# Eighteen full tiles of the first choice worked right behind attention, in a fused attention and mixture-of-experts block on Trainium2

## The chip, the cores and the metric

The kernel runs on one core of one Trainium2 chip. That core has TensorE (PE, with its weight load shown as PEld), VectorE (DVE), ScalarE (ACT), GpSimd (POOL) and SyncE (SP), and 16 DMA engines. PE multiplies, DVE, ACT and POOL work elementwise, SP and POOL issue most DMAs here. Each engine runs its own instructions in order, and waits at semaphores for the others. The metric is the device time of one execution in microseconds (us); less is better.

## The reference

The input x is 16 batches (B) of 512 tokens (L) with 128 channels (C). What is computed:

```
mod = (silu(c) @ wmod)                      # six vectors of 128 for each batch: sa ca ga sb cb gb
ga, gb = sign(.) * max(|.|, 0.25)
h = layernorm(x) * (1 + ca) + sa
x = x + ga * attention(h)                   # gather-conv: 8 heads, 32 taps each at learned offsets
h = layernorm(x) * (1 + cb) + sb
scores = h @ gate_w.T                       # 8 experts
the two best scores of each token, softmax over the two
y = sum over the two: share * ((silu(h1) * h2) @ w3[e].T),  h1, h2 = halves of h @ w12[e].T
x = x + gb * y
```

Only the two chosen experts of a token have to be worked. The kernel gathers each expert's tokens, and works the first choices of all tokens ("lo") before the second choices ("hi").

## The kernel before

**Attention.** The 16 batches are four groups (g) of four. A group has four head pairs (q) and two pairs of batches (p); a "cell" is one (g, q, p), 32 in all, and each takes nine steps. `attention()` writes out the order of the instructions by hand (no scheduler moves them): in each step it issues the cell's own work, and `between(s)` then places side work from four lists, `preparing`, `making`, `sorting` and `putting`, as far as the step's "room" in each engine lasts. The last cells are those of group 3.

**Dispatch.** What follows attention for a pair of batches is a `Dispatch` object. `make` is the out-projection (`multiply`, L1051), the residual (`add`, L1064), the second layernorm (`moments`, `root`, `scale`, `modulate`). `sort` transposes the result (L1109), multiplies by the gate weights (`scores`, L1115), ranks the eight scores (`ranks`, L1130 to L1142), picks two, computes their shares with a sigmoid, counts the tokens of each expert (`count`, PE) and adds them to the running count `run` (`places`): so each token has a row number in its expert's region, and pairs of batches must be counted one after another. `puts` are indirect DMAs on POOL's queue (`put`, L1225 to L1232), 128 rows each: for each pair of batches 8 to `lo_d` (130 numbers a row: share, place of the second choice, h) and 8 to `hi_d` (386 numbers: h, x, gb, share, token).

The pairs come out of attention in order. The last two are the pairs of group 3: the last but one ("pair 0") is made and sorted beside the last cells, as far as it gets, and the last (`last`) only after the last cell's `yg` (L989), whose rows it reads through `yl` (L1026). Behind attention stand, in this order: what is left of pair 0's sort, its 16 puts, the last pair's make and sort, its 16 puts, and `tile_table()` (L1303), 25 small DVE operations.

**Tiles.** An expert's rows are cut into tiles of 256 (MT). `tile_table` turns the counts into two tables of 38 entries (NTL) for lo and for hi: the row at which a tile begins and its expert, in `tab`, and the number of rows at its start to be skipped, in `sk` (a tile that would go past an expert's rows begins earlier and overlaps the one before).

**Experts.** The loop at the end of the kernel runs over pairs of tiles (TW = 2): 19 steps of lo, then 19 of hi. In a step: `front` has SP read a tile's address from the table and load its rows from `lo_d` or `hi_d` (one step ahead, L1569 to L1573); `load_lo` (hi only, L1582) loads the lo results from `yh_d`; `hidden` (L1613 to L1619) is the first product, silu and the gating; `turn` (L1600) transposes the next step's rows; `weights` has ACT copy the next step's two experts' weights; `output` (L1627) is the second product; `put_out` multiplies by the share and puts four times 128 rows out through indirect DMAs on POOL's queue (L1656): to `yh_d` in lo, to `out` in hi, after adding the lo results, gb and x. Rows, weights and results lie in a pool (`moe`) that is opened after attention's pool is closed.

For the program's semaphores, a DMA at an address read at run time counts as touching the whole of `lo_d`, `hi_d` or `yh_d`: a row load waits for all puts ahead of it in the program, and a put for all row loads ahead of it. The puts are written through separate views, so that they do not wait for one another.

## Time and profile before

| | us |
|---|---|
| median of 10 runs | 1428.37 (1421.17 to 1437.51) |
| the profiled execution | 1423.52 |
| its span (first to last instruction) | 1421.8 |
| PE busy, whole span | 1089.1 (77%) |
| DVE busy | 1083.5 (76%) |
| POOL busy | 808.0 (57%) |
| ACT busy | 739.8 (52%) |
| attention's last `yg` ends | 1117.0 |
| the first row load of lo is issued | 1167.7 |
| the steady steps of lo | 1185 to 1290 |
| the steady steps of hi | 1310 to 1405 |

The page gives busy times of each engine over the span, the granted TensorE clock as a share of full speed, and groups of instructions by line. The groups of the parts that matter here:

```profile
L1613 PE MATMUL hp<-h,wcp 128*128 128x256 f32 x608 | 140.9, 385 | 0.7 <-ACT h L1602 0.7
L1656 POOL DMA_INDIRECT yh_d<-o,to x76 | 74.7, 982 | 49.6 <-issue 17.7
L1656 POOL DMA_INDIRECT out<-o,to x76 | 74.9, 986 | 43.6 <-DVE o L1653 23.5
L1228 POOL DMA_INDIRECT lo_d<-wrow,at x64 | 64.2, 1004 | 47.5 <-issue 24.1
L1228 POOL DMA_INDIRECT hi_d<-wrow,at x64 | 63.5, 992 | 15.0 <-issue 14.3
```

A row reads: line, engine, operation, output and inputs, count, then busy time and mean nanoseconds of one, then the idle time of the engine just before these instructions and what ended most of it. Busy time of a DMA instruction on POOL is that of its issue; the data lands later. All times in the views below are from the span's start.

### The profile page before, as it was taken

Reading aid. Unit: us, or ns where it says so; the run is one execution under the profiler, and the core shown is the slowest. Engines: PE = TensorE matmul, PEld = TensorE weight load, DVE = VectorE, ACT = ScalarE, POOL = GpSimd, SP = SyncE. Lnnn points to the kernel's source line nnn. Section 1 sums busy time; section 2 is a strip of 40 time slices with the busy share of each in tenths; the row PEclk is TensorE's granted clock in tenths of the full one; section 3 lists DMA queues with packets and bytes.
Section 4 is the critical chain, followed back from the end, with each engine's and each line's share of the span. In section 5 each row is a group of like instructions: output and inputs, shape, how many; then the busy total and the mean of one; then the engine's idle time right before and its main releaser. Section 6 shows DMA issues by size and latency. Waiting matters only on the chain.

```text
span 1421.8 us, 21081 instructions
## 1 busy us (share of the span) xinstructions
PE 1089.1 (77%) x6422; PEld 460.1 (32%) x6422; DVE 1083.5 (76%) x1875; ACT 739.8 (52%) x1418; POOL 808.0 (57%) x851
## 2 busy tenths in 40 slices
PE   4377878886888788787888768877777419997995
PEld 2111212111222222212222222222212318996994
DVE  6587788787699889888899987878788743443775
ACT  5256655664564555654665545453544116564652
POOL 5555644443554386537844484754858354664666
PEclk9598999999998799879998998978988859998998
DMA  3353443444444333343344334443344223344772
GB/s 85 78 124 95 105 98 109 99 121 105 114 98 105 82 96 95 105 117 86 108 87 123 95 106 105 127 119 94 94 98 162 77 86 95 89 126 132 220 229 69
DMA packets 246863, 154.81 MB, mean 109 GB/s; under 512 B 169062, under 2 KB 217040, under 8 KB 246494
## 3 DMA queue, kind: packets, MB, share of 16 engines
q1 hardware_dynamic: 232300, 124.43, 33.9%
q0 software_dynamic: 13472, 28.37, 5.7%
q8 instruction: 51, 0.84, 0.3%
q10 hardware_dynamic: 978, 0.67, 0.2%
q14 instruction: 62, 0.51, 0.1%
HBM read 90.31 MB, written 64.09 MB: 109 GB/s over the span
## 4 chain that ended last, share of the span: by engine, by line
DVE 29%; PE 27%; issue 12%; ACT 11%; POOL 10%; DMA 7%; SPq 4%; POOLq 0%; ACTq 0%; DVEq 0%
DVE w L906 9%; DVE xx L908 8%; ACT n L870 6%; PE v L895 5%; PE hp L1613 4%; PE y L918 4%; POOL yh_d L1656 3%; PE v L866 3%; DMA wrow<-mod_d 3%; PE kp L513 2%; PE po L1627 2%; DVE ct L954 1%; PE kc L936 1%; ACT kc L888 1%; POOL nk L872 1%
## 5 line engine op out<-in xcount | busy, mean ns | idle before, releaser
L872 POOL TENSOR_SCALAR nk<-n 128x1024 int16<-128x1024 uint8 x256 | 270.8, 1058 | 399.1 <-ACT n L870 394.3
L870 ACT ACTIVATE n<-v 128x1024 uint8<-128x1024 f32 x256 | 261.9, 1023 | 291.8 <-PE v L866 282.7
L906 DVE SCALAR_TENSOR_TENSOR w<-v,kc 128x1024 f32<-128x1024 f32 x256 | 311.3, 1216 | 110.1 <-PE v L895 95.4
L908 DVE SCALAR_TENSOR_TENSOR xx<-v,w 128x1024 f32<-128x1024 f32 x256 | 313.4, 1224 | 8.8
L918 PE MATMUL y<-xx,dz 128*32 128x512 f32 x1024 | 300.5, 668 | 12.3 <-DVE xx L908 12.1
L918 PE MATMUL y<-w,zi 128*32 128x512 f32 x1024 | 302.4, 668 | 0.0
L895 PE MATMUL v<-nk,negn 128*128 128x512 f16 x512 | 174.3, 426 | 114.6 <-ACT n L870 83.1
L888 ACT COPY kc<-kt 128x128 f32<-128x128 f32 (+1 forms) x288 | 142.8, 496 | 162.4 <-DVE w L906 154.4
L866 PE MATMUL v<-rw,vt 32*128 32x512 bf16 x576 | 120.0, 413 | 63.2 <-DVE xx L908 61.0
L895 PEld LDWEIGHTS <-negn 128*128 128x128 bf16 x512 | 31.1, 99 | 351.4 <-ACT n L870 258.2
L1613 PE MATMUL hp<-h,wcp 128*128 128x256 f32 x608 | 140.9, 385 | 0.7 <-ACT h L1602 0.7
L1619 DVE TENSOR_TENSOR hid<-sl,hp 128x512 f32<-128x512 f32 x76 | 52.1, 686 | 116.9 <-ACT sl L1618 116.9
L1613 PEld LDWEIGHTS hp<-h,wcp 128*128 128x128 f32 x608 | 114.4, 194 | 15.9 <-ACT h L1602 1.1
L1656 POOL DMA_INDIRECT yh_d<-o,to x76 | 74.7, 982 | 49.6 <-issue 17.7
L1656 POOL DMA_INDIRECT out<-o,to x76 | 74.9, 986 | 43.6 <-DVE o L1653 23.5
L866 PEld LDWEIGHTS <-vt 32*128 32x128 bf16 x576 | 28.3, 92 | 202.7 <-DVE xx L908 96.4
L1228 POOL DMA_INDIRECT lo_d<-wrow,at x64 | 64.2, 1004 | 47.5 <-issue 24.1
L1618 ACT ACTIVATE sl<-hp 128x512 f32<-128x512 f32 x76 | 45.4, 597 | 87.0 <-PE hp L1613 87.0
L513 PE MATMUL kp<-hT,kw 128*128 128x512 f32 x128 | 80.3, 717 | 6.5 <-ACT cn L945 5.1
L1627 PE MATMUL po<-wcp,hid 128*128 128x128 f32 x608 | 76.1, 279 | 1.0 <-DVE hid L1619 1.0
L1627 PEld LDWEIGHTS po<-wcp,hid 128*128 128x128 f32 x608 | 72.7, 196 | 1.6 <-DVE hid L1619 1.5
L1228 POOL DMA_INDIRECT hi_d<-wrow,at x64 | 63.5, 992 | 15.0 <-issue 14.3
(272 smaller groups left out, 1655.9 us busy)
## 6 DMA issues: line engine op xcount, KB each, us to landing
row<-hi_d SPq DMA_DIRECT2D x38, 386.0 KB
kd<-ev SPq DMA_DIRECT2D x56, 256.0 KB
zi<-z_d SPq DMA_DIRECT2D x128, 64.0 KB
y_d<-yg SPq DMA_DIRECT2D x31, 256.0 KB
yl<-y_d SPq DMA_DIRECT2D x120, 64.0 KB
row<-lo_d SPq DMA_DIRECT2D x38, 130.0 KB
yl<-yh_d SPq DMA_DIRECT2D x38, 128.0 KB
xin<-in_x SPq DMA_DIRECT2D x8, 512.0 KB
```

The costliest lines, as they stand in the source:

```text
L866: T.matmul(v[:, n, :], vt[g, j, :], self.rw[n][g], start=True, stop=True)
L870: S.activation(n8, v, AF.Relu)
L872: G.tensor_scalar(self.new, n8, 64.0, 64.0, ALU.mult, ALU.add)
L888: S.copy(self.kc.rearrange("p n (c r) -> p n c r", r=BW)[:, :, :, r0 : r0 + nr], src)
L895: T.matmul(self.v[:, n, :], negn, prev[:, n, :].bitcast(F16), start=False, stop=True, skip_group_check=True,)
L906: V.scalar_tensor_tensor(w, v, -0.5, self.kc, ALU.is_gt, ALU.mult)
L908: V.scalar_tensor_tensor(xx, v, TIE + 0.5, w, ALU.add, ALU.mult)
L918: T.matmul(self.y[o : o + 32], self.zt[n][k][:, r, :], m[:, n, :], start=(r == 0), stop=(r == BW - 1), skip_group_check=True,)
L1228: G.indirect_dma_start(views[name][self.b0 * NT + k], bass.IndirectOffsetOnAxis(ap=self.at[:, s, k : k + 1], axis=0), self.w[n][:, i, o : ...
L1613: T.matmul(hp[:, m, here], t["wc"][w][:, o : o + P], hT[:, here], start=True, stop=True, skip_group_check=True,)
L1627: T.matmul(po[:, i, :], hid[:, n, i * P : (i + 1) * P], t["wc"][i // MI][:, o : o + C], start=(n == 0), stop=(n == FF // P - 1),)
L1656: G.indirect_dma_start(dst, bass.IndirectOffsetOnAxis(ap=at[:, i, :], axis=0), o[:, i, :], None, bounds_check=(E * REG - 1, B * L - 1)[ph] ...
```

## The change

After twelve batches (three groups) are sorted, some tiles of the first choice are already full with rows of those batches. A second, smaller table (`early_table`) is computed when the third group's last pair is sorted, inside attention: it lists the first 18 (EARLY) such tiles. Right behind attention nine steps of lo run on these 18 tiles (`experts` with `beside_early`), and the last pair's make, the sorts of the last two pairs and the lo puts of pair 0 are placed among them in pieces, at two places in each step, by lists and "room" as in attention. What is left in the lists is then issued in one go (`drain`): the rest of the last pair's sort, `tile_table`, its 8 lo puts. Then the other ten steps of lo run (`experts` with `beside_rest`), with the 16 hi puts of the last two pairs (a new list, `far`) among them, and at the end the 19 steps of hi. Row loads are issued two steps ahead in place of one. The lo steps' buffers are taken over from tiles of attention; the `moe` pool, now for hi alone, is opened after the last lo step. `tile_table` subtracts the tiles that `early_table` used, counted in `used`, and is cut into four pieces. The bodies of `front`, `load_lo`, `weights`, `turn`, `hidden`, `output` and `put_out` (now `puts_out`) are the same but for where their tiles lie.

```diff
+EARLY = 18
...
+    tail = []
+
+    def dtile(name):
+
+        return ps_y.tile([P, L], FP, tag="y", name=name) if tail else mtile(name)
+
...
-                Work(lambda n=n, k=k: self.multiply(n, k), 6 * int(n == k == 0), pe=0.8, dve=0.4)
+                Work(lambda n=n, k=k: self.multiply(n, k), 0 if last else 6 * int(n == k == 0), pe=0.8, dve=0.4)
...
-            if last:
-                for n in range(2):
-                    out += [Work(lambda n=n: self.scale(n, True))]
-                    out += [Work(lambda n=n, k=k: self.modulate(n, k, e)) for k in range(2)]
-                    out += [Work(lambda n=n: self.transpose(n)), Work(lambda n=n: self.scores(n))]
...
-        def puts(self):
+        def puts(self, which=(0, 1)):
             return [
                 Work(lambda k=k, s=s: self.put(k, s), int(k == s == 0), pool=1.3)
-                for s in range(2) for k in range(2 * NT)
+                for s in which for k in range(2 * NT)
...
+    def early_table():
+
+        fl = const.tile([P, 1, E], FP, name="fl")
+        box = {}
+
+        def first():
+            area.extend([cell.tile([P, 2 * NT * E * E], FP, tag="ge", name="ge", bufs=1), 0])
+            V.memset(used, 0.0)
+            cnt = const.tile([P, 1, E], FP, name="cnta")
+            V.tensor_tensor(cnt, run[:, 0:1], reg0[:, 0:1], ALU.subtract)
+            whole(fl, cnt, 0.0)
+
+        def second():
+            upto = box["upto"] = ends_of(fl, 1)
+            here = used[:, 0:1]
+            V.tensor_tensor(here, fl, upto, ALU.subtract)
+            V.tensor_scalar(here, here, float(EARLY), 0.0, ALU.add, ALU.max)
+            V.tensor_tensor(here, here, fl, ALU.min)
+
+        def third():
+            ef, sums = regions(box["upto"][:, 0], 0, EARLY)
+            bs = sk[:, 0, 0:EARLY]
+            sums(bs, fl[:, 0, 0 : E - 1])
+            V.tensor_tensor(bs, kf[:, 0:EARLY], bs, ALU.subtract)
+            V.tensor_scalar(bs, bs, float(MT), None, ALU.mult)
+            V.scalar_tensor_tensor(bs, ef, float(REG), bs, ALU.mult, ALU.add)
+            V.tensor_copy(tab[:, 0, 0, 0:EARLY], bs)
+            V.tensor_copy(tab[:, 0, 1, 0:EARLY], ef)
+            V.memset(bs, 0.0)
+            area.clear()
+
+        return [Work(first, dve=0.9), Work(second, dve=1.2), Work(third, dve=2.0)]
...
+        def tiles(s):
+            o = (EARLY, 0)[s]
+            n = NTL - o
+            sks = sk[:, s, o:NTL]
+            ef, sums = regions(box["upto"][:, s], o, n)
+            sums(sks, dt[:, s])
+            V.tensor_tensor(sks, kf[:, 0:n], sks, ALU.subtract)
+            V.tensor_scalar(sks, sks, used[:, s, 0:1], float(MT), ALU.add, ALU.mult)
+            bs = table_tile("bs", n)
+            sums(bs, dc[:, s])
+            V.tensor_scalar(bs, bs, cnt[:, s, 0:1], -float(MT), ALU.add, ALU.add)
+            V.scalar_tensor_tensor(bs, bs, 0.0, sks, ALU.max, ALU.min)
+            V.tensor_tensor(sks, sks, bs, ALU.subtract)
+            V.scalar_tensor_tensor(bs, ef, float(REG), bs, ALU.mult, ALU.add)
+            V.tensor_copy(tab[:, s, 0, o:NTL], bs)
+            V.tensor_copy(tab[:, s, 1, o:NTL], ef)
+
+        return [Work(first, dve=1.1), Work(second, dve=1.1)] + [
+            Work(lambda s=s: tiles(s), dve=3.0) for s in range(2)
+        ]
...
+            sorting.items += d.sort()
+            if (g, p) == (NG - 2, NP - 1):
+                sorting.items += early_table()
+
+            def goes():
+                putting.items.extend(d.puts((0,) if ahead else (0, 1)))
+                if ahead:
+                    far.items.extend(d.puts((1,)))
+                put_done.append(d)
+
+            sorting.items += [Work(goes)]
...
+    def front(ph, k):
+
+        width = (2 + C, 3 * C + 2)[ph]
+        t = dict(ph=ph, k=k, wc=[], at=[])
+        row = t["row"] = (
+            after[0].tile([P, NT, width], FP, tag="row1", name="row1", bufs=6) if ph else lo["row"][k % 4]
+        )
...
+    def buffers():
+
+        h, kt = groups[-1].hT.rearrange("p b c r -> p (b c r)"), kts[1].rearrange("p s n t -> p (s n t)")
+        last_pr = prm.rearrange("p t q r -> p (t q r)").bitcast(FP)
+        kc = cell.tile([P, 2, L], FP, tag="kc", name="rowa", bufs=1).rearrange("p n l -> p (n l)")
+        m, wide = NT * (2 + C), 2 * FF + FF // P * C
+        lo["row"] = [
+            t.rearrange("p (i w) -> p i w", i=NT) for t in [h[:, m * n : m * n + m] for n in range(3)] + [kc[:, 0:m]]
+        ]
+        lo["wc"] = [kt[:, wide * n : wide * n + wide] for n in range(5)] + [last_pr[:, 0:wide]]
+        lo["x"] = [cell.tile([P, 2, L], FP, tag="xx", name="xa") for _ in range(2)]
...
+    def experts(tiles, side=lambda: None):
+        tiles, rows = list(tiles), []
+
+        def fetch():
+            if tiles:
+                rows.append(front(*tiles.pop(0)))
+
+        fetch()
+        fetch()
+        cur, old = rows.pop(0), None
+        weights(cur)
+        turn(cur)
+        while cur or old:
+            fetch()
+            nxt = rows.pop(0) if rows else None
+            if cur:
+                if cur["ph"]:
+                    load_lo(cur)
+                hidden(cur, 0)
+            if nxt:
+                turn(nxt)
+                weights(nxt)
+            side()
+            if old:
+                output(old)
+            if cur:
+                hidden(cur, 1)
+            if old:
+                puts_out(old)
+            side()
+            cur, old = nxt, cur
+
+    step = [total + 2]
+
+    def beside_early():
+        flush()
+        for e, k in dict(pe=0.8, dve=2.0, act=1.2, pool=1.3).items():
+            room[e] = min(room[e] + k, k)
+        room["bank"] = 1
+        for line in (sorting, making, putting):
+            line.step(step[0], room)
+        step[0] += 1
+
+    def beside_rest():
+        room["pool"] = min(room["pool"] + 1.3, 1.3)
+        room["bank"] = 1
+        far.step(step[0], room)
+        step[0] += 1
+
...
-        flush()
-        paced.clear()
         cs[-1].take()
         cs[-1].finish(V)
-        making.drain()
-        sorting.drain()
+        flush()
         last.load_last()
-        putting.drain()
-        for w in last.make(True) + last.sort(True):
-            w.fn()
-        for w in last.puts():
-            w.fn()
-        tile_table()
+        buffers()
+        tail.append(True)
+        making.last = -9
+        making.items += last.make(True) + [Work(
+            lambda: sorting.items.extend(last.sort() + tile_table() + [Work(
+                lambda: (putting.items.extend(last.puts((0,))), far.items.extend(last.puts((1,))))
+            )])
+        )]
+        experts([(0, k) for k in range(EARLY // TW)], beside_early)
+        for line in (making, sorting, putting):
+            line.drain()
+        paced.clear()
+        experts([(0, k) for k in range(EARLY // TW, NTL // TW)], beside_rest)
+        far.drain()
+        attn_scope.close()
+        after.append(pool("moe", 2))
+        experts([(1, k) for k in range(NTL // TW)])
...
-    tiles = [(ph, k) for ph in range(2) for k in range(NTL // TW)]
-    with tc.manual_schedule(engines={ET.PE, ET.Activation, ET.DVE, ET.Pool, ET.SP}):
-        cur, old = front(*tiles[0]), None
-        weights(cur)
-        turn(cur)
-        for n in range(len(tiles) + 1):
-            nxt = front(*tiles[n + 1]) if n + 1 < len(tiles) else None
-            if cur:
-                if cur["ph"]:
-                    load_lo(cur)
-                hidden(cur, 0)
-            if nxt:
-                turn(nxt)
-                weights(nxt)
-            if old:
-                output(old)
-            if cur:
-                hidden(cur, 1)
-            if old:
-                put_out(old)
-            cur, old = nxt, cur
```

## The prediction

> **What bounds the kernel now.** I read first the windows by stage, then the chain of waits between attention and the experts, then the timelines of PE and POOL there. Windows (stretch, its length, then busy time of PE, PEld, DVE, ACT and POOL with instructions, granted clock, DMA share, GB/s):
>
> ```profile
> 1060.00:1110.00 50.00, 37.20 (x249) 13.58 (x249) 42.99 (x66) 25.65 (x52) 37.05 (x37) 0.90 0.48 149
> 1110.00:1170.00 60.00, 15.99 (x140) 12.42 (x132) 36.32 (x119) 7.55 (x24) 27.30 (x28) 0.61 0.22 70
> 1185.00:1290.00 105.00, 105.00 (x662) 96.14 (x660) 43.93 (x110) 62.48 (x128) 70.48 (x72) 1.00 0.32 94
> 1290.00:1310.00 20.00, 11.39 (x55) 9.84 (x55) 5.41 (x14) 5.33 (x11) 4.19 (x5) 0.74 0.50 146
> 1310.00:1405.00 95.00, 93.97 (x595) 86.00 (x594) 70.97 (x151) 54.51 (x111) 64.14 (x66) 1.00 0.69 205
> ```
>
> The expert stages are bound by PE: 100% and 99% busy at full clock, 5.68 us a step (one pair of tiles; hp starts 1184.29 and 1189.96). The 60 us after attention hold 16.0 us of PE work: that hole is what can be filled, with a second one of 20 us between lo and hi. Chain of waits (start, duration, what):
>
> ```profile
> 1116.27 0.69 DVE yg L989
> ...
> 1146.32 0.70 DVE ge L1130
> ...
> 1164.84 2.43 DMA lo_d<-wrow,at
> 1167.65 0.36 SPq L1573
> ...
> 1168.83 2.06 DMA row<-lo_d
> ...
> 1289.28 2.17 DMA yh_d<-o,to
> ...
> 1303.23 0.34 SPq L1573
> 1304.35 3.83 DMA row<-hi_d
> ```
>
> Attention ends with yg at 1116.96; the last pair's sort starts at 1146.32, its puts land at 1167.27, and only then the first row load goes out. So a put that a row load waits for costs from 1164.84 (put begins) to 1170.89 (second half of the row landed): **6.05 us**. Timeline of POOL, first puts of the experts:
>
> ```profile
> 1189.46 1.00 POOL L1656 DMA_INDIRECT yh_d<-o,to  x1 [13.48 <-ACT sl L1618]
> 1190.77 0.99 POOL L1656 DMA_INDIRECT yh_d<-o,to  x1 [0.30 <-issue]
> 1192.06 0.98 POOL L1656 DMA_INDIRECT yh_d<-o,to  x1 [0.30 <-issue]
> 1193.35 0.98 POOL L1656 DMA_INDIRECT yh_d<-o,to  x1 [0.31 <-issue]
> ```
>
> Back to back, a put takes 1.285 us of POOL's queue (1.29 here; 1.27 from 1155.39 on, for lo_d and hi_d alike), whatever its width. Four fill 5.14 of a step's 5.68 us: POOL has room for **less than half a put more per step**. That decides this case.
>
> **The change, part by part** (span time; before's span is 1421.8, its execution 1423.52, the median of the runs 1428.37, 0.34% above the execution).
>
> *a. The early table in attention.* 21 small DVE operations and two memsets, behind the sort of the third group's second pair, some 17 of attention's steps before its end. At 0.20 us for 8-wide and 0.28 to 0.33 for 128-wide operations (sort chain, 1149.46 to 1154.37) they are 5.4 us on a DVE that is 86% busy (42.99 of 50). Between 0 (all in its 7 idle us) and 5.4; I take half, 2.7. Last yg: 1119.7.
>
> *b. Start of the early tiles.* SP issues the four yl loads behind yg first (2.42 us, they sit in its queue ahead), then the first row load, 0.83 later: 1122.9.
>
> *c. Filling the pipe.* From the first row load to the first yh put before took 1167.65 to 1189.46 = 21.8. Added: the last-but-one pair's sigmoid falls among the silus, two more table loads on ACT, 1.28 each as at 1173.93, with its count on PE: 0 to 3.6, I take 2.4. First yh put 1147.1.
>
> *d to g. The moved puts, and their queue.* The last-but-one pair's 8 lo puts were issued at 1123.79 to 1134.05 beside the last pair's make, where POOL had nothing to do, and cost nothing. Now they stand among the early steps' yh puts: one in the first loop, then two a loop. They write lo_d, the row loads read it, both at addresses known only at run time. So each row load waits for the lo puts ahead of it in program order, and each lo put for the row loads ahead of it. With loads two steps ahead, POOL's queue reads: yh(0) x4, put 1; put 2 (waits for the load of step 4, which waits for put 1), yh(1) x4, put 3; put 4 (waits for the load of step 5, which waits for puts 2 and 3), yh(2) x4, put 5; and so on to put 8. Everything behind a waiting put waits too, the yh puts above all; and PE's turn of step 4, 5, 6, 7, 8 waits for that row. A round: put to row landed 6.05 (up to 7.8 if the row takes the 3.83 us that the hi row took; I take 6.9, the middle), then put, four yh puts, next put's start, 5 x 1.285 = 6.43, and 0.1 for the wait: **13.4 us a loop in place of 5.68**. First yh puts 4 x 1.285 = 5.14, put 1 starts 1152.3; step 4's row at 1159.2; three rounds, 40.2 (37.7 to 43): step 7's at 1199.4; step 8's, 6.9 + 0.2: 1206.5. The last pair's make and its transposes lie inside these loops, under POOL's waits, at no cost; without that cover its make is the 30 us that it took before.
>
> *h, i. The last pair's sort.* Turn of step 8, its hidden and output, the scores behind them: some three loops' PE work, 19 (17 at 5.68 a step; 25 at the clock of 0.74). Sort starts 1225.5. From there nothing of step 9 can run: sort to first lo put 1146.32 to 1155.39 = 9.07, eight puts, landing, first row load 1155.39 to 1167.65 = 12.26 (table inside it): 1246.9. The hole after the sort is not filled, it is **moved behind the early tiles**.
>
> *j. The pipe fills a second time:* 21.8 again, first yh put of step 9 at 1268.7.
>
> *k. The deferred hi puts.* 16 hi puts, before at 1134.36 to 1144.4 and 1166.11 to 1175.98 under other work, now stand in the queue of the 10 last lo steps. Three go ahead of it; then 40 yh + 13 hi = 53 x 1.285 = 68.1, mostly six a step, 7.7 against PE's 5.68. Last put starts 1335.5; the first hi row load reads hi_d and its yl reads yh_d, and the new pool waits for all of it: + 2.2 landing + 0.4 = 1338.1.
>
> *l. The hi stage is as before:* from its first row load to PE's end of two steps 18.45 (as at 1167.65 to 1186.1), 17 x 5.68 = 96.6, tail 1402.6 to 1421.8 = 19.2: 134.2. The lo to hi transition lost 12.4 before (1286.51 to 1310.29 = 23.78 for two steps of 5.68); before's first hi row load was ahead of the last yh puts, now it isn't.
>
> Sum 1338.1 + 134.2 = **1472.3**, 50.5 above 1421.8; on the median 1428.4 + 50.5 = **1479**. Own range: lower ends together about -11, upper ones +14: 1468 to 1493.
>
> The granted clock was 0.61 and 0.74 in the two holes and 1.00 in the steady stages, and the first eight hp matmuls took 3.78 us where sixteen later took 3.62. [...]
>
> The lo_d put took 2.43 us until it had landed. [...]
>
> **The rivals.**
>
> *B, the ping-pong hides* (0.17; median 1454): the loads' two steps of lead cover the put's landing, and POOL only carries its puts: four loops at 6 x 1.285 = 7.71, the others at 5.68. Sort starts at 1147.1 + 8 x 5.68 + 4 x 2.03 = 1200.6, 24.9 earlier. For: a lead of two steps is 11.4 us, a round 6.05. Against: the lead is spent, since the put that a load waits for waits itself for the load before.
>
> *C, the other side: not slower* (0.10; 1429): POOL's queue rate is not what sets the pace, because a put beside matmuls issues faster. It decides from six puts per 5.68 us, 0.95 each, on. Then no stage leaves PE's pace: sort at 1147.1 + 45.4 = 1192.5, step 9's first put + 21.4 + 21.8 = 1235.7, last put + 9 x 5.68 + 3.9 = 1290.7, hi load 1293.3, end 1427.5; with a's and c's 5.1 hidden too, 1422.4, 0.6 above before. For: busy time of a put is 0.98. Against: no two puts in the timeline come closer than 1.27.
>
> *D, worse* (0.13; 1500): PE stays at the gated clock through the stalled loops and both drains, rows land in 3.83: h at 25 (+6.0), two fills at 25 (+6.4), five rounds at 7.8 (+4.5), the upper ends of a and c (+3.9): 1472.3 + 20.8 = 1493.1. Against: a loop's PE work at half rate is 11.4, still below the round's 13.4.
>
> That the change does not do what it says is in the sum: only the last pair's make and scores overlap the early tiles, its ranks, places and puts run alone (h, i).
>
> **How the numbers follow.** The forecast has 0.60, B 0.17, C 0.10, D 0.13. What this kernel's measurement can tell from no change is about 0.5%, 7 us: C gives 0.05 faster and 0.05 same; the others, 0.90, are slower. The range runs from B less 8, 1446 (its own terms are as uncertain as the forecast's), to D less 4, 1496: C and the ends of the others are left out.
>
> **What would show it.** Right: on POOL in the early loops, second lo puts idle before them, released by the row load, and PE idle some 7 us in each of five loops; POOL back to back at 7.7 us a step in the last lo steps, with hi puts among them; two stretches of over 20 us with PE below half busy, after the early tiles and before hi. Wrong: early loops at 5.7 or 7.7 us (B), POOL with idle gaps in the last lo steps (C), the first row of step 9 before the sort's end, or hi rows ahead of the last yh put.

## The result, and the profile after

The changed kernel takes 1490.34 us (median of 13 runs, 1485.52 to 1498.85), beside 1428.07 (46 runs) for the kernel before: the ratio is **1.0445, interval 1.0427 to 1.0464**, 62.3 us slower. The forecast was 50.5 us slower, 1479 in a range of 1446 to 1496. The profiled execution took 1488.56 us, its span is 1486.8, against the sum's 1472.3.

Windows of the changed kernel (stretch, length, busy time of PE, PEld, DVE, ACT, POOL with instructions, granted clock, DMA share, GB/s), cut at the stages:

```profile
1132.00:1163.00 31.00, 20.79 (x112) 17.65 (x113) 7.25 (x21) 13.84 (x29) 0.00 (x0) 0.67 0.17 44
1163.00:1222.00 59.00, 40.05 (x209) 35.09 (x207) 20.98 (x77) 20.67 (x44) 27.52 (x28) 0.83 0.18 55
1222.00:1242.00 20.00, 16.00 (x93) 14.25 (x91) 8.30 (x21) 6.43 (x13) 11.95 (x12) 0.82 0.10 41
1242.00:1283.00 41.00, 17.27 (x103) 13.90 (x104) 19.18 (x72) 11.45 (x27) 14.77 (x15) 0.63 0.20 60
1283.00:1352.00 69.00, 44.75 (x287) 40.98 (x286) 20.80 (x53) 26.71 (x55) 52.01 (x53) 0.87 0.27 88
1352.00:1375.00 23.00, 17.19 (x85) 14.53 (x86) 4.74 (x10) 9.04 (x19) 0.00 (x0) 0.73 0.74 241
1375.00:1470.00 95.00, 93.97 (x595) 85.99 (x595) 72.24 (x152) 54.54 (x112) 63.90 (x66) 1.00 0.64 194
```

Before, PE was 100% busy through all of the steady lo steps. Now only the last row, the hi steps, is such a stage. The early steps (second and third row) have PE two thirds to four fifths busy at a granted clock of 0.83. Then comes a hole of 41 us with 17.3 us of PE work: the one that stood behind attention, moved behind the early tiles. In the fifth row POOL issues 53 indirect DMAs in 69 us and PE is busy for 44.8.

POOL's timeline in the changed kernel (start, duration, what; in brackets the idle time before it and what ended it):

```profile
1181.67 0.97 POOL L1235 DMA_INDIRECT lo_d<-wrow,at  x1 [0.30 <-issue]
1188.21 0.97 POOL L1235 DMA_INDIRECT lo_d<-wrow,at  x1 [5.58 <-DMA hT<-lo_d]
1189.48 1.00 POOL L1687 DMA_INDIRECT yh_d<-oa,to  x1 [0.30 <-issue]
...
1193.36 0.98 POOL L1687 DMA_INDIRECT yh_d<-oa,to  x1 [0.30 <-issue]
1194.64 0.97 POOL L1235 DMA_INDIRECT lo_d<-wrow,at  x1 [0.30 <-issue]
1201.29 0.97 POOL L1235 DMA_INDIRECT lo_d<-wrow,at  x1 [5.67 <-DMA hT<-lo_d]
...
1287.28 0.98 POOL L1687 DMA_INDIRECT yh_d<-oa,to  x1 [0.30 <-issue]
1288.56 0.97 POOL L1235 DMA_INDIRECT hi_d<-wrow,at  x1 [0.30 <-issue]
1289.84 0.97 POOL L1235 DMA_INDIRECT hi_d<-wrow,at  x1 [0.30 <-issue]
1291.12 1.00 POOL L1687 DMA_INDIRECT yh_d<-oa,to  x1 [0.30 <-issue]
```

The first block is the ping-pong. The put at 1194.64 starts at once, the next one waits 5.67 us until a row load (hT is the tile that the row lands in) has run, and that load waits for the put at 1194.64: 1201.29 less 1188.21 is a loop of 13.1 us. The second block is a step of the later lo tiles: two hi puts between the yh puts of two steps, with nothing but the 0.30 us of issue between them.

The chain of waits of the changed kernel (start, duration, what), at one turn of the ping-pong, at the row load behind the second sort, and between lo and hi:

```profile
1181.67 2.29 DMA lo_d<-wrow,at
...
1184.16 0.34 SPq L1604
...
1185.35 2.05 DMA hT<-lo_d
1187.45 0.69 PE ntp L1631 x2
...
1259.52 2.28 DMA lo_d<-wrow,at
...
1350.28 2.09 DMA yh_d<-oa,to
...
1354.95 3.59 DMA row<-hi_d
```

Put, landing, load, landing, and PE at 1187.45, which waited for the row: 1181.67 to 1187.45 is 5.8 us. The same pair, put and row load, stands in the chain again at 1259.52, for the last of the last pair's lo puts, and the first hi row waits for the last yh put's landing.

### The profile page after: what moved, and what is told of

Same layout as the page of the kernel before. It is cut to its first block, busy times and chain, and to the rows that moved or that the text cites. A ratio compares the mean times of both kernels' runs of the same rounds, so it can differ in the third digit from the quotient of the medians.

```text
span 1486.8 us, 21113 instructions
## 1 busy us (share of the span) xinstructions
PE 1116.8 (75%) x6422; PEld 469.9 (32%) x6422; DVE 1091.5 (73%) x1908; ACT 746.3 (50%) x1426; POOL 807.5 (54%) x851
## 4 chain that ended last, share of the span: by engine, by line
PE 31%; DVE 30%; ACT 11%; issue 9%; DMA 7%; POOL 6%; SPq 4%; ACTq 0%; POOLq 0%; DVEq 0%
DVE w L907 10%; PE hp L1644 8%; DVE xx L909 8%; ACT n L871 6%; PE po L1658 4%; PE v L896 4%; PE y L919 3%; PE v L867 3%; PE kp L514 2%; DMA wrow<-mod_d 2%; DVE ct L955 2%; ACT kc L889 1%; ACT wrow L1100 1%; POOL nk L873 1%; POOL yh_d L1687 1%
## 5 line engine op out<-in xcount | busy, mean ns | idle before, releaser
L907 DVE SCALAR_TENSOR_TENSOR w<-v,kc 128x1024 f32<-128x1024 f32 x256 | 311.4, 1216 | 115.8 <-PE v L896 99.7
L919 PE MATMUL y<-xx,dz 128*32 128x512 f32 x1024 | 306.3, 680 | 11.4 <-DVE xx L909 11.3
L919 PE MATMUL y<-w,zi 128*32 128x512 f32 x1024 | 308.1, 680 | 0.0
L896 PE MATMUL v<-nk,negn 128*128 128x512 f16 x512 | 178.3, 434 | 111.7 <-ACT n L871 86.4
L1687 POOL DMA_INDIRECT yh_d<-oa,to x76 | 75.2, 990 | 88.8 <-DVE ms L1208 41.4
L1650 DVE TENSOR_TENSOR hida<-xa,hp 128x512 f32<-128x512 f32 x38 | 26.1, 686 | 111.4 <-ACT xa L1649 111.4
L1235 POOL DMA_INDIRECT hi_d<-wrow,at x64 | 63.3, 990 | 15.1 <-issue 14.5
L831 POOL TENSOR_TENSOR zi<-zi,hsel 128x288 f32<-128x288 f32 x64 | 58.1, 908 | 22.7 <-DMA zi<-z_d 22.6
L1644 PE MATMUL hp<-xa,kt 128*128 128x256 f32 x256 | 68.5, 408 | 1.8 <-ACT xa L1633 1.3
L1650 DVE TENSOR_TENSOR hid<-sl,hp 128x512 f32<-128x512 f32 x38 | 26.0, 684 | 53.9 <-ACT sl L1649 53.9
L1644 PE MATMUL hp<-h,kt 128*128 128x256 f32 x256 | 63.8, 390 | 0.8 <-ACT h L1633 0.8
L919 PEld LDWEIGHTS y<-xx,dz 128*32 128x32 f32 x1024 | 38.6, 113 | 79.0 <-issue 61.8
```

The costliest lines, as they stand in the source:

```text
L896: T.matmul(self.v[:, n, :], negn, prev[:, n, :].bitcast(F16), start=False, stop=True, skip_group_check=True,)
L907: V.scalar_tensor_tensor(w, v, -0.5, self.kc, ALU.is_gt, ALU.mult)
L919: T.matmul(self.y[o : o + 32], self.zt[n][k][:, r, :], m[:, n, :], start=(r == 0), stop=(r == BW - 1), skip_group_check=True,)
L1235: G.indirect_dma_start(views[name][self.b0 * NT + k], bass.IndirectOffsetOnAxis(ap=self.at[:, s, k : k + 1], axis=0), self.w[n][:, i, o : ...
L1644: T.matmul(hp[:, m, here], t["wc"][w][:, o : o + P], hT[:, here], start=True, stop=True, skip_group_check=True,)
L1687: G.indirect_dma_start(dst, bass.IndirectOffsetOnAxis(ap=at[:, i, :], axis=0), o[:, i, :], None, bounds_check=(E * REG - 1, B * L - 1)[ph] ...
```

## The experiments

They ran on four chips, numbered 2, 5, 6 and 15 on record. On chip 2 the kernel before takes 1426 us, near the 1428 of the result, whose chip has no number on record; on chips 5, 6 and 15 it takes 1479 to 1480. The expectations call chip 2 the first or the faster one, and the other three the second or the slower one. Each ratio is to runs of the kernel before on the same chip. The diffs are against the changed kernel unless another is named. "From the last yg" means from the end of attention's last `yg` in the profile.

**The puts and their queue.** Three edits: the early lo puts left for after the early tiles, so that nothing writes `lo_d` while rows are loaded (first); all 16 hi puts issued in the drain, while PE waits anyway, instead of among the last lo steps (second); and both.

```diff
# lo puts late
-        for line in (sorting, making, putting):
+        for line in (sorting, making):
# hi puts in the drain
-        for line in (making, sorting, putting):
+        for line in (making, sorting, putting, far):
```

> The changed kernel, but the 8 lo puts of the last-but-one pair leave the early loops: they are issued behind the ninth early step, ahead of the last pair's 8. Ping-pong theory: no early row load waits for a put any more, the early loops go at PE's pace: first yh puts of step 0 to step 8 take 8 x 5.68 = 45 us in place of 78.7 (1163.4 to 1242.1), 33 less; the 8 puts cost some 7 in the drain (8 x 1.27 less the 3.5 us that POOL idled ahead of it). Net -26: about 1464 us. Rival, the puts themselves or the gated clock hold the loops: 8 puts off POOL there, 8 more later, about 1488 to 1490.

> The changed kernel, but the 16 deferred hi puts are all issued right behind the last pair's lo puts, ahead of the ten last lo steps, in place of among them. POOL theory: 13 x 1.28 = 16.7 us of puts fit into the 19.1 us in which POOL idled before the first yh put of step 9; the last lo steps then go at 5.68: step 9's first yh put to the last one's start is 9 x 5.68 + 3.9 = 55 us in place of 66.9. Net -12: about 1478 us. Rival, PE or the row loads set these steps' pace and POOL only looks full: no change, 1490.

> Both edits of the two runs before. If the two POOL terms are separate they add: -26 - 12 = -38, about 1452 us, still above before's 1428, by the drain and second filling (43 us in the changed kernel) and the emptying between lo and hi. If one hides the other, the sum is smaller than its parts: 1464 or more.

Measured on chip 5: 1528.4 (ratio 1.0329, 1.0285 to 1.0372), 1532.2 (1.0335, 1.0285 to 1.0386), 1530.0 (1.0321, 1.0267 to 1.0376). The changed kernel itself was not among these runs, and the three are not told apart by their times. Their profiles say more, since each edit is missing in one of them. From step 0's first yh put to step 8's took 78.6 us in the second run, and 63.1 and 63.2 in the two without the early puts. From step 9's first yh put to the last took 81.1 in the first run, and 62.1 and 64.9 in the two without the hi puts. So both edits shorten their stage. What eats the gain is the drain between the two stages: 51.4, 54.4 and 64.9 us, where a kernel with neither edit (the padded one below, on chip 15) takes 41.3. In the third run the first four row loads behind the last pair's puts go out over 21.8 us; on chip 2, with the same edits, over 4.1. What holds them back on chip 5 was not found. So the question went to chip 2, with the changed kernel beside it.

> The changed kernel unedited, as the measure for the three others of this comparison, since the chip of the comparison before worked the kernel before in 1479 us, 3.6% more than the first one's 1428. As on the first chip: ratio 1.0445, if the terms do not depend on the chip. If a chip whose granted clock falls in the steady expert steps has less to lose by POOL's queue, the ratio is smaller.

> The 8 lo puts of the last-but-one pair issued behind the early steps, as in the first of these experiments, beside the changed kernel itself. Ping-pong theory by the profile: the early loops lose the puts' round, but steps 1 to 3 still wait for the last pair's out-projection (PE waits there for the PSUM bank that DVE frees): step 0's to step 8's first yh put 63 us in place of 78.7, as measured, and the drain 8 us less, not more, as the last lo put starts at 119.0 after the last yg in place of 127.4: in all about -15 against the changed kernel. Rival (the prediction's full 33 less 7): -26. Rival (no gain): 0.

> Lo puts late and hi puts in the drain, beside the changed kernel itself: -15 from the first and -12 from POOL's rate in the last lo steps, less what the 32 puts in one row cost ahead of step 9 (its first yh put came at 159.4 after the last yg in place of 145.8): -12 to -15 in all. If they were additive as the prediction has it: -27 or more.

| on chip 2 | us (median) | ratio and interval | step 0's first yh put to step 8's | to step 9's | step 9's to the last yh put | last yg to end |
|---|---|---|---|---|---|---|
| changed | 1489.06 | 1.0423 (1.0369 to 1.0476) | 78.5 | 41.4 | 67.0 | 355.0 |
| lo puts late | 1476.17 | 1.0358 (1.0311 to 1.0404) | 56.4 | 48.1 | 67.0 | 338.4 |
| both | 1461.31 | 1.0257 (1.0214 to 1.03) | 56.3 | 48.5 | 54.0 | 325.2 |

Without the ping-pong the early loops take 22.1 us less. The drain behind them gets 6.7 longer, since eight more puts of 1.27 us stand ahead of the last pair's. The medians lie 12.9 us apart; the intervals of the two ratios overlap, so it is the stage times that show what hangs on the place of eight puts (the early loops took 78.5 to 78.7 us in all four profiles of kernels with these puts in place). The second edit takes another 14.9 us, and here the intervals do not overlap: the later lo steps go from 67.0 to 54.0, and the drain stays as it was, so the hi puts are hidden there. The expectation for both together had been set too low after chip 5's runs; the prediction's own arithmetic, 53 puts against 9 to 10 steps of PE, was right. Windows of the run with both edits (columns as above):

```profile
1165.00:1220.00 55.00, 45.76 (x281) 40.65 (x279) 27.85 (x85) 24.75 (x52) 30.66 (x32) 0.94 0.19 61
1220.00:1268.00 48.00, 17.81 (x105) 14.44 (x106) 19.32 (x73) 11.68 (x27) 34.93 (x36) 0.60 0.36 116
1268.00:1322.00 54.00, 44.54 (x285) 40.77 (x284) 20.15 (x52) 26.36 (x54) 38.23 (x39) 0.94 0.21 65
```

The 285 matmuls of the last row are those that took 69 us in the changed kernel (287 there, 44.75 us of PE): the same PE work with 13 fewer puts between the first yh put and the last, and 12.9 us less from the one to the other. The first row falls short of the dense steps: 281 matmuls are 45.76 us, and the eight loops take 7.0 us each on average where 5.68 was expected. One loop of 12.2 us makes most of that; the others take 5.3 to 7.3. In the long one PE stops twice for the last pair's out-projection (PE's timeline of the same run; brackets as before):

```profile
1170.15 1.13 PE L1058 MATMUL po<-ow,yl 128*128 128x128 f32 x8 [2.90 <-DVE wrow L1064]
...
1174.84 1.13 PE L1058 MATMUL po<-ow,yl 128*128 128x128 f32 x8 [1.40 <-DVE wrow L1064]
```

It takes its results through one kind of PSUM buffer, and the next product waits until DVE has read the last one.

**What attention lost.** The table alone, added to the kernel before at the same place and not used for anything:

```diff
# against the kernel before
-            sorting.items += d.sort() + [Work(lambda: (putting.items.extend(d.puts()), put_out.append(d)))]
+            sorting.items += d.sort()
+            if (g, p) == (NG - 2, NP - 1):
+                sorting.items += early_table()
+            sorting.items += [Work(lambda: (putting.items.extend(d.puts()), put_out.append(d)))]
```

> The kernel before with early_table alone: its 23 DVE operations behind the sort of the third group's second pair, their result unused, all else as before. In the two profiles attention ended 15.1 us later in the changed kernel. Theory of the prediction: the table costs 0 to 5.4 us, 2.7 the middle: about 1431 us, ratio 1.002 (at most 1.004); the rest of the 15 us lay ahead of the table, where both kernels issue the same instructions, and differs from run to run. Rival, the table (its late landing, the order behind it) costs attention the most of it: 1438 to 1443, ratio 1.007 to 1.011.

Measured on chip 5: 1486.1 beside 1479.2, ratio 1.0054 (1.0025 to 1.0083), 8 us with an interval of 3.7 to 12.3, between what the theory (at most 1.004) and its rival (1.007 to 1.011) had expected. In its profile the stretch from the yg of cell 28 to the last yg, in which the table lies, takes 99.7 us; before it took 92.9 and in the changed kernel 99.1 (98.2 to 102.9 in the other profiles with the table). Timelines of DVE and POOL in the table's run:

```profile
1050.20 0.15 DVE L1358 TENSOR_TENSOR cnta<-run,reg 128x8 f32<-128x8 f32 x1
...
1051.71 0.97 DVE L1364 TENSOR_TENSOR used<-fl,upto 128x8 f32<-128x8 f32 x1
1052.72 0.17 DVE L1365 TENSOR_SCALAR used<-used 128x8 f32<-128x8 f32 x1
1052.93 0.17 DVE L1366 TENSOR_TENSOR used<-used,fl 128x8 f32<-128x8 f32 x1
1055.41 1.26 DVE L1335 TENSOR_TENSOR ge<-upto,kf 128x126 f32<-128x126 f32 x1
1056.70 0.28 DVE L1340 TENSOR_REDUCE ge<-ge 128x18 f32<-128x126 f32 x1
...
1058.48 0.07 DVE L1377 MEMSET sk<- 128x18 f32 x1
...
1051.63 1.05 POOL L873 TENSOR_SCALAR nk<-n 128x1024 int16<-128x1024 uint8 x1 [2.14 <-ACT n L871]
...
1055.25 1.27 POOL L990 TENSOR_TENSOR yg<-ys,fs 128x512 f32<-128x512 f32 x1 [2.57 <-ACT fs L988]
```

The 21 operations (two of them memsets) lie in two closed stretches, 1050.20 to 1053.10 and 1055.41 to 1058.55, of 6.0 us together. The delay, 6.8 us here and 6.3 in the changed kernel, is at least their whole length: none of it went into DVE's idle time. The two long ones (0.97 and 1.26 us) began while POOL worked on an elementwise operation, and ended within 0.2 us of its end, 1052.68 and 1056.52; in the changed kernel they do the same (0.97 and 1.25 us, with ends at 1066.01 and 1069.98 beside POOL's 1065.99 and 1069.83). That they waited for POOL is the likely reading, which no run tests.

That leaves a part that the table does not explain, since the table comes later in time. In the changed kernel the cells fall behind from the first on, although each engine's instructions stand in the same order as before up to cell 29: 1.2 us at cell 0, 5 at cell 8, 8 at cell 24, and at cell 28, ahead of the table, 8.9 (POOL's timelines, before and after):

```profile
1024.07 1.27 POOL L989 TENSOR_TENSOR yg<-ys,fs 128x512 f32<-128x512 f32 x1
```

```profile
1032.95 1.28 POOL L990 TENSOR_TENSOR yg<-ys,fs 128x512 f32<-128x512 f32 x1
```

What differs there is where attention's buffers lie in SBUF. The small tables of the change are allocated ahead of them, and in the compiled kernel (the traces hold no addresses) the first of these buffers begins at byte 35456 of a partition before, a multiple of 64, and at 35872 after, 32 past one. The kernel with the table alone begins them at 35648, a multiple again. The differences, 416 and 192 bytes, are what the added and dropped small tables come to if each is rounded up to 32 bytes. So eight unused numbers, 32 bytes, were put in between:

```diff
     used = const.tile([P, 2, E], FP, name="used")
+    pad = const.tile([P, 8], FP, name="pad")
+    V.memset(pad, 0.0)
```

> The changed kernel with one more constant of 32 bytes per partition, and nothing else. In six profiles of the changed kernel and its variants the 28th cell's yg came 9 to 13 us later than in the kernel before, although the instructions up to there are the same, in the same order; in the run with the table alone it came 5 us earlier. The new constants move all other tiles: they begin 32 bytes past a multiple of 64 in the changed kernel and its variants, on a multiple of 64 in the kernel before and in the run with the table alone; and the 104,828 DMA packets of 256 bytes took 19.9 to 20.1 ns in place of 18.7 to 18.8. Theory (place of the tiles): with the constant the packets take 18.8 again, the 28th cell's yg comes at 1020 to 1028 in place of 1033 to 1037, ratio 1.034 to 1.037 in place of 1.042. Rival (the clock's pattern, by chance): as before, 1.042.

Measured on chip 15: 1529.2, ratio 1.0344 (1.03 to 1.0388). The changed kernel without the pad did not run on chips 5, 6 or 15, so what the pad is worth in the total is not shown. But in POOL's timeline of this run cell 28's yg is back:

```profile
1023.84 1.27 POOL L990 TENSOR_TENSOR yg<-ys,fs 128x512 f32<-128x512 f32 x1
```

Over all profiles of this study, this yg lies between 1019.2 and 1027.0 in the six with an address that is a multiple of 64, and between 1033.0 and 1036.8 in the eight without. The two groups do not meet, and on chip 5, which ran both, they lie at 1019.2 and at 1034.9 to 1036.8. The last yg of this run ends at 1123.0, against 1132.1 to 1139.6 without the pad. So the delay ahead of the table is shown to come from 32 bytes of placement: 8.9 us in the changed kernel, 11 to 13 between this run and chip 5's three without the pad. Only four addresses were tried, one of them no multiple of 64.

**Does the idea win without its stalls?** The next kernel is meant to take all stalls away at once. Four row loads go out first. Then pair 0's sort and its 16 puts run in one go, hidden behind those four steps. The last pair is made and sorted with more room (to the seventh loop), its 8 lo puts go out in one go, and all 19 lo steps are one loop, so that nothing is drained. The out-projection takes turns with a second kind of PSUM buffer.

```diff
...
+    def early_start():
...
+        for line in (sorting, putting, far):
+            line.drain()
...
+            for e, k in dict(pe=1.7, dve=2.6, act=2.0, pool=1.3).items():
+                room[e] = min(room[e] + k, k)
...
+    def last_goes():
+        for w in last.puts((0,)):
+            w.fn()
+        far.items.extend(last.puts((1,)))
...
-        experts([(0, k) for k in range(EARLY // TW)], beside_early)
...
-        experts([(0, k) for k in range(EARLY // TW, NTL // TW)], beside_rest)
+        experts([(0, k) for k in range(NTL // TW)], beside_lo, 4, early_start)
```

> The early tiles kept, but each set of lo puts issued in one batch where no row load has to follow it soon: four row loads go ahead, then the last-but-one pair's sort is ended and its 8 lo and 8 hi puts issued in one go while the pipe fills; the last pair's make and sort get more room in each loop and end by the seventh, its 8 lo puts follow in one go, and all 19 lo steps run in one loop without a drain. Theory (the loss is the ping-pong and the second filling, not the early tiles): sort and second filling, 43 us, and the ping-pong, 5 x 7.4 us, go, a stall of about 9 us for the one batch stays, lo is bound by POOL: 92 puts x 1.285 = 118 us from the first yh put, about 27 us after the first row load: span about 1400 to 1410 on the first chip, ratio 0.98 to 0.99. Rival (the early tiles themselves, their cold clock and their buffers, cost the time): still above before, 1.01 or more.

Measured on chip 2: 1432.91, ratio 1.0051 (1.0026 to 1.0076), between what the theory (0.98 to 0.99) and its rival (1.01 or more) had expected: the stalls were most of the loss, and with most of them gone the idea still does not win. From the last yg to the end it takes 297.6 us, beside 304.8 before and 355.0 for the changed kernel. So behind attention it gains 7.2 us, but its last yg ends at 1135.1, 18.1 later than before, by the table and the placement above: that is what leaves it slower. Its windows behind attention, its POOL at the first yh put, and PE at the batch of the last pair's puts:

```profile
1135.00:1171.00 36.00, 29.59 (x192) 25.67 (x192) 19.48 (x74) 18.68 (x43) 15.87 (x17) 0.86 0.35 103
1171.00:1222.00 51.00, 36.97 (x219) 32.32 (x219) 29.76 (x99) 21.59 (x47) 32.64 (x33) 0.83 0.24 73
1222.00:1300.00 78.00, 61.04 (x389) 55.88 (x387) 26.82 (x69) 36.28 (x74) 58.08 (x59) 0.93 0.26 83
```

```profile
1169.61 0.97 POOL L1241 DMA_INDIRECT hi_d<-wrow,at  x1 [0.31 <-issue]
1170.89 1.00 POOL L1693 DMA_INDIRECT yh_d<-oa,to  x1 [0.30 <-issue]
```

```profile
1216.63 1.19 PE L1650 MATMUL hp<-xa,kt 128*128 128x256 f32 x2 [7.58 <-DVE hida L1656]
```

The hole behind attention is filled now: 29.6 us of PE work in 36. The first yh put comes 35.8 us after the last yg, 36.7 earlier than before (72.5), and it waits for nothing but the puts ahead of it in POOL's queue. But of these 36.7 us only 7.2 are left at the end. Last yh put: 161.9 against 182.4, 20.5 earlier: in the third window POOL has 59 puts in 78 us, and 59 x 1.285 = 75.8 is a full queue, and at the batch PE stands still for 7.6 us. First put to `out`: 187.7 against 193.1, 5.3 earlier, because the first hi row waits for the last yh put (its load goes out at 1299.28, the put at 1296.94), while before it was 28 us ahead of it.

The last three try for the rest. One goes on without a break into hi: hi rows take over the buffers of the sort's rows, the other tiles stay those of lo, and two hi rows are loaded before lo's last puts (two row loads in front, and the pad). The next is the batched kernel with the pad, and with the last pair's copies out of PSUM issued at once, not one call later. The last is the first of these with four row loads in front and with the same earlier copies.

```diff
# one stream, against the batched kernel
-            after[0].tile([P, NT, width], FP, tag="row1", name="row1", bufs=6) if ph else lo["row"][k % 4]
+            wrows.tile([P, NT, WROW], FP, tag="wrow", name="row1")[:, :, 0:width] if ph else lo["row"][k % 4]
...
+        if n == 2 * (NTL // TW - 2):
+            far.drain()
+            pre.extend(front(1, k) for k in range(2))
...
-        after.append(pool("moe", 2))
-        experts([(1, k) for k in range(NTL // TW)])
+        experts([(1, k) for k in range(2, NTL // TW)], ahead=0, rows=pre)
```

> The batched version with three more edits: the constant of 32 bytes; two row loads in place of four ahead of the first lo puts, which then begin some 8 us earlier; and hi without a pool of its own, its rows in the four tiles that held the last pairs' rows, its other tiles those of lo, the first two hi rows loaded before lo's last yh puts, so that PE goes from lo to hi without a drain. From the last yg to the end the batched version took 297.6 us (before: 304.8). Theory (POOL's row of 108 puts and the drains are what is left): -8 for the puts' start, -15 to -20 for the drain (out's first put came 25.9 us after yh's last, 10.7 in the kernel before): 270 to 275 us behind the last yg, with attention as in the aligned run about 1395 to 1405 us, ratio 0.98 to 0.985. Rival (lo's end, where POOL is the bound, sets hi's start all the same): 285 us, ratio 0.99 to 1.00.

> The batched version again (four row loads first), with the constant of 32 bytes and with the last pair's copies out of PSUM issued at once, not one call later. Against the batched version (1.0051 on the faster chip): attention 10 to 12 us earlier as in the aligned run, and up to 5 us of PE's waits for these copies. On the faster chip 1417 to 1422 us, ratio 0.993 to 0.997; on the slower one, where PE's steps take 6.3 to 6.8 us and hide more of POOL's queue but less of the rest, about the same or up to 1.01. Rival (the batched version's remaining loss is not attention but the early tiles): 1.005 on either.

> The same with hi in one stream behind lo (rows in the last pairs' tiles, no pool of its own), four row loads first: the last run with two row loads first gave 1.0127 on the slower chip, where PE waited 3.7 and 2.6 us for the third row load and then went on at a low clock. Theory: the drain between lo and hi, 15 us more than in the kernel before, goes: 10 to 15 us below the run beside it, ratio 0.983 to 0.99 on the faster chip, on the slower one 0.99 to 1.00. Rival (what one gains at the drain PE loses to its clock or to four row tiles in place of six): no better than the run beside it.

Measured: one stream with two loads 1501.1 on chip 15 (1.0127, 1.0083 to 1.0171), batched and padded 1492.3 on chip 6 (1.0108, 1.0075 to 1.0142), one stream with four loads 1491.5 on chip 6 (1.0099, 1.0076 to 1.0122). None reaches the kernel before, and the gains that the theories of the first and the last expected did not come. The last two are not told apart. In the last the first hi row does go out 23.5 us before the last yh put, and the first `out` put follows it after 13.3 us instead of 26.5; but its hi steps then wait for their rows, 18.8 us of PE in 15 waits, and the steps from the first `out` put to the end take 154.7 us against 138.8. What the join gained is lost there. None of the three ran on chip 2.

No version that beats the kernel before was found. What the batched kernel with the pad would take on chip 2 can only be estimated: its attention on chip 6 (1126.2) and the 297.6 us of the batched one make a span of 1423.9, and with the padded changed kernel's attention (1123.0) 1420.6, against 1421.8 before. That is no gain that could be measured.

## Why the prediction was right, and where its terms were not

| the prediction's step | predicted | after |
|---|---|---|
| a: last yg ends | 1119.7 | 1132.1 |
| b: to the first row load | 3.25 | 3.80 |
| c: to the first yh put | 24.2 | 27.5 |
| d: to put 1 | 5.14 | 5.22 |
| e, f: put 1 to step 7's row | 47.1 | 45.7 |
| g, h: to the last pair's sort | 26.1 | 27.5 |
| i, j: sort to step 9's first yh put | 43.2 | 41.7 |
| k: to the last yh put | 66.8 | 66.9 |
| to the first hi row load | 2.6 | 2.4 |
| l: to the end | 134.2 | 134.1 |

Behind attention the sum was 352.6 us and the span has 354.7. Of the 14.5 us that the span lies above the forecast, 12.4 are term a. That the rest comes within 2.1 us is in part luck: its larger errors (+3.3 in c, -1.4 in e and f, +1.4 in g and h, -1.5 in i and j) partly cancel.

- **a, mis-sized.** The prediction put "half" of the table's 5.4 us, 2.7, on the path; it cost 6.3, all of it and more than the upper bound, since two of its operations took 0.97 and 1.25 us where the rows for such widths had 0.17 and 0.28. (They are 19 operations and two memsets; the prediction counted 21 and two.) The 14% that DVE was idle was no cover: in attention DVE and PE wait for each other, as two rows of the changed kernel's groups say (columns as in the groups shown of before). w waits for PE's v, and PE's next v for xx, so what is put between them would move both; this reading is argued from the rows. The other 8.9 us, the buffers' place in SBUF, were in no term at all.

```profile
L907 DVE SCALAR_TENSOR_TENSOR w<-v,kc 128x1024 f32<-128x1024 f32 x256 | 311.4, 1216 | 115.8 <-PE v L896 99.7
...
L867 PE MATMUL v<-rw,vt 32*128 32x512 bf16 x576 | 122.5, 422 | 65.0 <-DVE xx L909 62.9
```

- **c, mis-sized by 3.3 us.** Its sigmoid and table loads were counted at 2.4; filling the pipe beside the sort and the make took 5.7 more than before.
- **e and f, right.** Three loops took 12.98, 13.08 and 12.98 us, 13.4 predicted; the rows landed in 2.05 to 2.12 us, as the one before had (2.06), and not in the 2.9 that the middle implied. The put's landing was 2.28 to 2.31 us, where the row before had 2.43. That the ping-pong is the cause is shown by moving the puts. What it cost in all is less than the loops suggest: 22.1 us, where the eight loops' 78.5 less 8 x 5.68 would be 33.1, because loops without it take 7.1 us on average (56.4 / 8), and not the 5.68 of dense steps: the last pair's out-projection, which the ping-pong had covered, then stops PE itself.
- **g to j, right:** the sort, ranks, places and puts of the last pair run alone (41.7 us with PE at 17.3), and the pipe fills twice. (The upper value for h, 25 at a clock of 0.74, is mis-worked: 17 over 0.74 is 23. It enters rival D alone.)
- **k, right,** and shown: with 13 puts fewer in the queue these steps take 54.0 us on chip 2, and the puts taken out cost nothing in the drain there.
- **Rival B** (the loads' lead hides the landing) is out: the second put of each loop waits 5.6 us. **Rival C** (POOL's rate does not matter) is out: no two indirect DMAs came closer than 1.26 us, and the later lo steps got shorter when 13 puts left them. **Rival D** held in one point, the clock of 0.83 in the early loops (what it calls the gated clock is the lower one of the records, 0.50 from 1131 to 1178 in the kernel before), and its price did not appear, since POOL's wait covers it: eight hp matmuls took 3.78 us behind attention's pause, ten took 2.32 in the loop at 1190.88, and the loops still took 13.0. D's total is near the result by another cause: its surplus was in h, the fills and the rounds, and the run's is in attention.

## What to carry to other kernels

Work that is moved into a hole brings its stores with it. Here the stores wrote the tensor that the hole's loads read, both at addresses known only at run time: store and load waited for each other in turn, 13.0 us a loop where a dense step takes 5.68, and a lead of two loads was used up at once (the second put of each loop waited 5.6 us). So put such stores out in one batch, with enough loads ahead of it, and count every store against the queue's rate in the stage that it goes to (1.285 us a put here; with 13 puts fewer the later lo steps went from 67.0 to 54.0 us). When a change adds small buffers, compare a stretch that the change does not touch: if it got slower too, as here by 8.9 us, look at the addresses before looking for a reason in the code.

## What the runs showed of the hardware that was not expected

- **32 bytes of placement.** The 104,828 packets of 256 bytes in the first 1050 us took 18.7 to 18.8 ns each on average where attention's buffers begin at a multiple of 64 bytes, and 19.9 to 20.1 ns where they begin 32 past one, in all 14 profiles. 1.2 ns on each is 126 us over 16 DMA engines, 8 us for one: the size of the delay, but that the packets are its cause is only argued.
- **Stops on three of the chips, and the clock of PE follows them.** On chip 15 the steady hi steps of the padded kernel have a granted clock of 0.89, where the same steps have 1.00 in the first fence (window with the columns as above):

```profile
1390.00:1485.00 95.00, 77.60 (x439) 70.30 (x436) 52.70 (x110) 40.93 (x85) 49.46 (x50) 0.89 0.55 166
```

  In 95 us 439 matmuls run there, against 595 in the last row of the first fence, so the clock alone does not explain the loss. About every third step takes 9 to 11 us in place of 5.7. Timelines of PE, ACT, DVE and PE again in one of them:

```profile
1386.38 3.62 PE L1646 MATMUL hp<-h,kt 128*128 128x256 f32 x16
...
1386.82 0.40 ACT L1626 COPY kt<-w_sb 128x256 f32 x1
1393.78 1.09 ACT L1651 ACTIVATE sl<-hp 128x512 f32<-128x512 f32 x2 [6.56 <-remote]
...
1394.41 0.69 DVE L1652 TENSOR_TENSOR hid<-sl,hp 128x512 f32<-128x512 f32 x1 [6.74 <-ACT sl L1651]
...
1395.15 3.36 PE L1660 MATMUL po<-kt,hid 128*128 128x128 f32 x14 [4.49 <-DVE hid L1652]
```

  By its records PE was done with the hp products at 1390.0, but ACT's `sl` on them start only at 1393.78, both back to back; the profile names no releaser ("remote"). DVE waited for `sl`, and PE for DVE. The same steps of this run and of four others (three on chip 5, one on chip 6) have 25 such places, always at the same matmuls of the program, 108 matmuls or three steps apart. In 24 of the 25 PE stops for 2.4 to 4.6 us, once for 1.1; on chip 2 it has no gap there. So their distance belongs to the program and not to a time. Which engine stopped first, and why, stays open: the profiles from chips 5, 6 and 15 also hold fewer semaphore updates (21,100 to 21,900, beside 25,200 to 25,400 in the others). What they do show is the order of stop and clock. In those 24 the half clock, 3.4 or 6.8 us long, begins 2.0 to 5.3 us after PE's stop begins, so there the low clock follows the stops and does not make them.
- **Indirect puts have one rate.** 128, 130 or 386 numbers a row, to `lo_d`, `hi_d`, `yh_d` or `out`: nine in ten take 0.96 to 1.02 us, with 0.30 of issue behind it, and single ones up to 1.5. In all 14 profiles no two start closer than 1.26 us.
